# Picking the first unit's search rows with TensorE in a four-stage transformer kernel

## The chip, the core and the metric

The kernel runs on one core of a Trainium2 chip. A core has five engines, each working through its own list of instructions in order: TensorE for matrix products (PE in the profile, with its weight loads listed apart as PEld), VectorE (DVE), ScalarE (ACT), GpSimd (POOL) and SyncE (SP). In this kernel SP does nothing but issue DMA transfers, which 16 DMA engines of the core carry out. The metric is the device time of one launch in microseconds; less is better. The output has to agree with the reference.

## What is computed

A block with four residual stages on `x` of 2048 x 256:

```python
x = x + xcond0(layernorm(x), ctx, ctx, tau, delta, Wq, bq, Wk, bk, Wv, bv, Wo, bo)
x = x + top1_of_8_experts(layernorm(x), ...)
x = x + local_attention(ctx, layernorm(x), ...)
x = x + slot_layer(layernorm(x), ...)
```

The change lies in the first stage, cross attention of 2048 queries with 1601 keys in 16 heads of 16 columns:

```python
qh = (q @ Wq.T + bq).reshape(B, L, H, E)
kh = (k @ Wk.T + bk).reshape(B, S, H, E)
vh = (v @ Wv.T + bv).reshape(B, S, H, E)
scores = einsum('blhe,bshe->bhls', qh, kh) * tau + delta
a = softmax(scale * scores)
out = einsum('bhls,bshd->blhd', a, vh).reshape(B, L, D) @ Wo.T + bo
```

## The kernel before

**Units.** Queries go in 4 blocks of 512 (`LB`), heads in 4 groups of 4 (`NG`), so the attention is 16 units, each one block with one group. A unit has two passes. The *search* (`largest`, L242) finds each query's largest score by matmuls on bfloat16 copies and a VectorE maximum; the largest scores, negated and split in two parts, become two rows of the query operand. The *exact pass* (the loop of L676 to L725) then takes scores in float32r, exponentials on ScalarE, and the weighted sum. In the loop, unit `u`'s exact pass runs beside the searches of later units. Only unit 0's search has no exact pass beside it, so the loop can't start until that search has ended.

**Row operands.** Each number is split: for the search in two bfloat16 parts (`k1`, `k2`; `one_two` for queries), for the exact pass in two float32r parts (`khi`, `klo`; `hi_lo`). An operand holds three rows for each of the 16 columns of a head (high, high, low against high, low, high), four heads on the partitions in two halves (`HR` = 64) and two planes, then two rows for `delta` (`ROW_OFF`), then, in `qt`, two for the negated maximum. `kb[g]`, `qb` are the search operands and `kt[g]`, `qt`, `ql` the exact ones. A part is made with one column on each partition, so that rows have to move between partitions. All of that is done by DMA: the search parts are stored into DRAM (`store_rows`, L215: `k_rows`, `q_rows`) and fetched back in the row layout (`fetch_rows`, L225); `khi` and `klo` are copied to `kt[g]` from memory to memory on the chip, 12 transfers of 16 rows for a group (`spread`, L421); `qt` and `ql` are fetched from `q_rows` (`fill`, L225 and L504). `offsets` (L365 to L376) writes the two `delta` rows of all groups of `kb` and the four of `kt` by transfers whose destination has two or four partitions.

**Order.** The stage has its order written out by hand. SP has one queue: its transfers start in the order in which the code issues them, an instruction of SP waits for the data it sends, and it waits too until the transfer eight places ahead has landed, since eight semaphores go round. The opening is: loads; constants; layer norm of block 0; keys of columns 0 to 127 (`keys`, L390); their search parts stored; queries of the first half (L471); the rest of SP's list; then unit 0's search, 32 steps of two 402-column score tiles (matmuls L262, maximum L266). Between the steps the list `rest` is popped: queries of the second half, keys of columns 128 to 255 (`other_keys`, `more_keys`), `spread_others`, and `values` (L432, L438). After the last step `least` and `turned` (L278 to L300) put the negated maximum into `qt[0]` (the transfers `qt<-nT`, last in SP's list of the stage), and the loop's first score matmul (L720) waits for them.

**Buffers.** PSUM has eight banks: here two double tiles `two()`, one double `big()`, and one single `small()`; the eighth bank is unused until the loop's `acc`. `ew`, the expert weights, is loaded late (unit 2), and rows 12 to 15 of `x_sb` are loaded once the loop has begun.

Of the kernel before, what the change touches and what calls it, by code (L numbers as in the profile page):

```python
# [19 lines left out]
P = 128  # L20
# [42 lines left out]
def body(ctx: ExitStack, tc: tile.TileContext, a: dict, out: bass.AP):  # L63
# [3 lines left out]
    work = ctx.enter_context(tc.tile_pool(name="work", bufs=4))  # L67
# [23 lines left out]
    def layer_norm_stats(src, n, rows=P):  # L91

        stats = work.tile([P, 4, 6], F32, name="ln_stats")
        mv = work.tile([P, 4, 2], F32, name="ln_mv")
# [4 lines left out]
        ve = work.tile([P, 4], F32, name="ln_ve")  # L99
        nc.vector.tensor_scalar_add(ve[:rows, :n], mv[:rows, :n, 1], EPS)  # L100
        rstd = work.tile([P, 4], F32, name="ln_rstd")
# [38 lines left out]
    def load_experts():  # L140
# [4 lines left out]
        rev_i = work.tile([P, 1, NE], I32, name="rev_i", bufs=1)  # L145
# [33 lines left out]
    with (  # L179
# [136 lines left out]
        with tc.tile_pool(name="proj", bufs=1) as proj:  # L316
# [27 lines left out]
            nc.vector.memset(raw(qt[0]), 1.0)  # L344
            nc.vector.memset(raw(ql[0]), 0.0)
            for n in range(2):
                nc.vector.memset(qb[n], 1.0)
            nc.gpsimd.memset(v, 1.0)
# [5 lines left out]
            for n in range(1, nq):  # L354
                nc.vector.memset(raw(qt[n]), 1.0)
                nc.vector.memset(raw(ql[n]), 0.0)
# [6 lines left out]

            def offsets():
                nc.vector.tensor_scalar_mul(d, d, 0.25)  # L365
                nc.vector.memset(raw(off_t), 1.0)
                for off in (off_b, off_t):
                    nc.vector.tensor_copy(off[:, 0, :], d)
                    nc.vector.tensor_tensor(off[:, 1, :], d, raw(off)[:, 0, :], ALU.subtract)
                for rows, off in zip(off_rows, (off_t, off_b)):  # L370
                    nc.sync.dma_start(rows.rearrange("w (p j) -> p w j", p=P), raw(off))
                for rows, dst in zip(off_rows[::-1], (kb_all, kt_all)):
                    n = rows.shape[0]
                    for h in range(2):
                        r = h * HR + ROW_OFF
                        nc.sync.dma_start(  # L376
                            raw(dst[r : r + n]).rearrange("r g l s -> r (g l) s"),
                            rows[:, :SP].unsqueeze(1).to_broadcast([n, 2 * NG, SP]),
                        )
# [4 lines left out]
            k2 = proj.tile([P, SP], BF16, name="k2")  # L384

# [29 lines left out]
            def spread(g):  # L415

                for w, t in ((1, khi), (2, khi), (0, klo)):
# [8 lines left out]
            def values(i0, i1):  # L426

                ps = two()
                for i in range(i0, i1):
                    n = srows(i)  # L430
                    for c in range(2):
                        nc.tensor.matmul(  # L432
                            ps[:n, i - i0, :D], ctxT[:, c, i * P : i * P + n], wv[:, c, :],
                            start=c == 0, stop=c == 1,
                        )
                for i in range(i0, i1):
                    n = srows(i)
                    nc.scalar.copy(  # L438
                        v[:n, i, : H * VW].rearrange("p (h r) -> p h r", r=VW)[:, :, :E],
                        ps[:n, i - i0, :D].rearrange("p (h r) -> p h r", r=E),  # L440
                    )

            def block(lb):
# [23 lines left out]
                for n in range(2):  # L467
                    def project(n=n):
# [6 lines left out]
                        b = bq[:, n : n + 1]  # L475
                        for t in (one_two, hi_lo):
# [3 lines left out]
                        search, rows = q_rows[1][lb % 2][n], q_rows[0][lb % 2][n]  # L480
                        store_rows(search, slice(0, W, 2), one_two[0])
                        store_rows(search, slice(1, 2), one_two[1])
                        store_rows(rows, slice(0, 2), hi_lo[0])
                        store_rows(rows, slice(2, 3), hi_lo[1])

                    yield project

# [22 lines left out]
            first[0]()  # L510
            ps_of = [two() for _ in range(2)]
            for half in range(2):
                for part in range(2):
                    keys(0, half, part, ps_of[half])
                first_keys(0, half, ps_of[half], k1)
                second_keys(0, half, ps_of[half], k1, k2)
                store_search_keys(0, slice(half * 2 * CH, (half + 1) * 2 * CH))
            fetch_search_keys(0)
            for step in first[1:6]:
                step()  # L520
            fill_search(0)
            for half in range(2):
                first_keys(0, half, ps_of[half], khi)
            for half in range(2):
                second_keys(0, half, ps_of[half], khi, klo)
            spread(0)
            fill(0)
            fill_search(1)
            fetch_search_keys(1)
            fill(1)  # L530
            spread(1)


            rest = [first[6]]

            def other_keys(half):
                ps_of[half] = two()
                keys(1, half, 0, ps_of[half])

            def more_keys(half):  # L540
                keys(1, half, 1, ps_of[half])
# [819 lines left out]
```

## Time and profile before

| | us |
|---|---|
| median of 3 runs | 1127.58 |
| lowest, highest | 1123.11, 1133.59 |
| the profiled execution, its own time | 1131.35 |
| its span | 1129.6 |
| PE busy in the span | 964.9 (85%) |
| DVE busy | 729.0 (65%) |
| ACT busy | 501.1 (44%) |

Where the opening stands in the profiled execution, in us from the span's start:

| event | at |
|---|---|
| first key matmul (L390) | 5.89 |
| SP issues the fetch of `kb[0]` | 36.08 |
| first search matmul of unit 0 (L262) | 44.81 |
| last maximum of unit 0 | 107.17 |
| first exact matmul of the loop (L720) | 112.42 |

How to read it: the attention loop ends near 833 us and the other three stages fill the rest. A profile's row gives an operation as `out<-in`, its count and its busy time, then in brackets the idle time before it and who ended it. In a table of windows, "busy" is of the window's length, PEclk is the share of full clock that TensorE was granted, and the DMA share is the mean over the 16 DMA engines: 0.25 may mean that four of them are at work and twelve are idle.

### The profile page before, as it was taken

To read this page: it belongs to the slowest core of one execution; us is meant where nothing else is said; L and a number is where in the kernel's file an instruction comes from. 1 tells how busy PE (TensorE), PEld (TensorE's weight loads), DVE (VectorE), ACT (ScalarE), POOL (GpSimd) and SP (SyncE) were. 2 spreads that over 40 slices of the span, in tenths; PEclk is the share of its full clock that TensorE was granted. 3 is DMA by queue.
4 is the path that set the end of the run, shared out by engine and by line. 5 is a ranking of instruction groups with operands and counts; after the bars stand their busy time and mean duration, and the time that the engine had idled before them with its cause. 6 is when DMAs were issued, how large, how long until landed. Compare 5 with 4: busy or idle time off the path is not lost.

```text
span 1129.6 us, 14408 instructions
## 1 busy us (share of the span) xinstructions
PE 964.9 (85%) x5593; PEld 445.9 (39%) x5593; DVE 729.0 (65%) x1382; ACT 501.1 (44%) x579; POOL 53.5 (5%) x78
## 2 busy tenths in 40 slices
PE   5337878999988899988899999989999999998856
PEld 2114333444433344443334444343334364644524
DVE  5245667888775688867688876867025647656433
ACT  2011454666655566655566665655840011221320
POOL 1000200000010000001000000000020001011100
PEclk8568798999999899999999999998999999999765
DMA  5777212210002111010310110100043000000002
GB/s 155 160 174 140 78 43 69 59 45 26 28 1 69 42 28 27 2 26 12 100 27 2 27 27 1 28 1 1 1 115 103 1 0 1 1 1 0 1 1 74
DMA packets 33182, 47.83 MB, mean 42 GB/s; under 512 B 6530, under 2 KB 22347, under 8 KB 32859
## 3 DMA queue, kind: packets, MB, share of 16 engines
q1 hardware_dynamic: 31338, 44.48, 14.9%
q10 hardware_dynamic: 1232, 1.61, 0.4%
q0 software_dynamic: 544, 0.82, 0.3%
q8 instruction: 44, 0.72, 0.3%
q14 instruction: 24, 0.19, 0.1%
HBM read 27.66 MB, written 14.04 MB: 37 GB/s over the span
## 4 chain that ended last, share of the span: by engine, by line
PE 63%; DVE 24%; issue 5%; DMA 5%; ACT 2%; SPq 1%; POOL 0%; POOLq 0%; DVEq 0%; ACTq 0%
PE acc L676 18%; DVE mx L266 16%; PE a_ps L262 10%; PE s_ps L720 10%; PE y_ps L855 8%; PE a_ps L239 2%; DVE ln_stats L96 2%; DMA k_rows<-k 2%; PE s_ps L432 1%; PE tr_ps L816 1%; PE f_ps L1273 1%; PE s_ps L390 1%; PE o_ps L1038 1%; DVE x_sb L862 1%; PE a_ps L651 1%
## 5 line engine op out<-in xcount | busy, mean ns | idle before, releaser
L266 DVE TENSOR_REDUCE mx<-a_ps 128x1 f32<-128x402 f32 (+1 forms) x661 | 488.9, 781 | 141.3 <-PE a_ps L262 137.3
L725 ACT ACTIVATE es<-s_ps 128x1024 f32<-128x1024 f32 (+1 forms) x416 | 406.2, 1021 | 250.6 <-PE s_ps L720 237.3
L262 PE MATMUL a_ps<-kb,qb 50*128 50x402 bf16 x992 | 214.6, 346 | 72.9 <-DVE mx L266 30.8
L720 PE MATMUL s_ps<-qt,kt 52*128 52x512 f32 (+1 forms) x832 | 233.2, 519 | 2.1 <-DMA qt<-nT 2.1
L676 PE MATMUL acc<-es,v 128*32 128x512 f32 (+1 forms) x1664 | 230.5, 626 | 0.0
L262 PEld LDWEIGHTS <-qb 50*128 50x128 bf16 x1024 | 75.6, 94 | 332.6 <-issue 294.6
L720 PE MATMUL s_ps<-ql,kt 52*128 52x512 f32 (+1 forms) x832 | 187.6, 400 | 0.0
L720 PEld LDWEIGHTS s_ps<-qt,kt 52*128 52x128 f32 (+1 forms) x832 | 89.1, 187 | 50.4 <-ACT es L725 27.3
L720 PEld LDWEIGHTS s_ps<-ql,kt 52*128 52x128 f32 (+1 forms) x832 | 99.8, 189 | 0.3
L855 PE MATMUL y_ps<-expert_wT_sb,xT 128*128 128x512 f32 x192 | 89.6, 606 | 0.0
L862 DVE SCALAR_TENSOR_TENSOR x_sb<-y_ps,r_gate,x_sb 128x256 f32<-128x256 f32 x96 | 46.3, 483 | 47.4 <-PE y_ps L855 45.4
L676 PEld LDWEIGHTS acc<-es,v 128*32 128x32 f32 (+1 forms) x1664 | 33.3, 109 | 50.0 <-issue 48.4
L102 POOL TENSOR_TENSOR ln_rstd<-ln_ve,mhalf 128x4 f32<-128x4 f32 (+1 forms) x17 | 17.5, 1032 | 700.1 <-DVE ln_ve L100 700.1
L819 ACT COPY xT<-tr_ps 128x512 f32<-128x512 f32 x22 | 12.7, 584 | 84.9 <-PE tr_ps L816 84.9
L855 PEld LDWEIGHTS y_ps<-expert_wT_sb,xT 128*128 128x128 f32 x192 | 35.3, 194 | 35.5 <-issue 34.0
L625 DVE RECIPROCAL rec<-a_ps 128x16 f32<-128x16 f32 x16 | 4.1, 257 | 52.2 <-PE a_ps L239 52.2
L855 PE MATMUL y_ps<-expert_wT_sb,xnT 128*128 128x512 f32 x64 | 32.4, 633 | 0.0
L816 PE MATMUL tr_ps<-ident,xn 128*128 128x128 f32 x88 | 20.3, 330 | 12.6 <-DVE xn L107 12.3
L314 DVE SCALAR_TENSOR_TENSOR qp<-a_ps,cols,qp 128x512 bf16<-128x512 f32 x8 | 6.0, 751 | 32.8 <-ACT qhi L310 32.8
L862 DVE SCALAR_TENSOR_TENSOR x_sb<-y_ps,gate,x_sb 128x256 f32<-128x256 f32 x32 | 15.4, 482 | 13.4 <-PE y_ps L855 12.8
L816 PEld LDWEIGHTS tr_ps<-ident,xn 128*128 128x128 f32 x88 | 13.0, 159 | 27.0 <-DVE xn L107 15.3
L310 ACT ACTIVATE qp<-a_ps,cols 128x512 bf16<-128x512 f32 x8 | 5.5, 687 | 40.3 <-PE a_ps L471 40.3
(288 smaller groups left out, 689.1 us busy)
## 6 DMA issues: line engine op xcount, KB each, us to landing
qt<-q_rows SPq DMA_DIRECT2D x32, 192.0 KB
q_rows<-qhi SPq DMA_DIRECT2D x8, 512.0 KB
kt<-khi SPq DMA_DIRECT2D x32, 100.5 KB
qb<-q_rows SPq DMA_DIRECT2D x32, 96.0 KB
kb<-k_rows SPq DMA_DIRECT2D x8, 301.5 KB
q_rows<-qp SPq DMA_DIRECT2D x8, 256.0 KB
q_rows<-qlo SPq DMA_DIRECT2D x8, 256.0 KB
ql<-q_rows SPq DMA_DIRECT2D x32, 64.0 KB
```

The source lines that it names most:

```text
L96: nc.vector.bn_stats(stats[:rows, i, :], src[:, i, :])
L102: nc.gpsimd.tensor_tensor(rstd[:rows, :n], ve[:rows, :n], mhalf[:rows, :n], ALU.pow)
L239: nc.tensor.transpose(ps[:, t * P : (t + 1) * P], src[:, t, c * P : c * P + n], ident)
L262: nc.tensor.matmul(ps[:, k, :CH], qb[u % 2][rows, pl, t * P : (t + 1) * P], kb[g][rows, pl, c * CH : (c + 1) * CH], start=True, stop=True,)
L266: nc.vector.tensor_reduce(flat[:, n : n + m], ps[:, :m, :CH], AX.X, ALU.max)
L676: nc.tensor.matmul(acc[HP * j : HP * (j + 1), :], v[:n, i, h * VW : h * VW + HP], es[j // 2][:n, j % 2, :], start=i == 0, stop=i == NS - 1,)
L720: nc.tensor.matmul(ps[:n, h, :], kt[u % NG][rows, pl, i * P : i * P + n], q[u % nq][rows, pl, :], start=k == 0, stop=k == 1,)
L725: nc.scalar.activation(e[:n], ps[:n], AF.Exp)
L816: nc.tensor.transpose(ps[:, t * P : (t + 1) * P], xn[:, t, c * P : (c + 1) * P], ident)
L819: nc.scalar.copy(xT[:, c, :], ps)
L855: nc.tensor.matmul(ps.rearrange("p e d -> p (e d)"), xT[:, c, tok], ew[:, c, pair * 2 * D : (pair + 1) * 2 * D], start=c == 0, stop=c == 1,)
L862: nc.vector.scalar_tensor_tensor(xb[:, t, :], ps[:, k, :], gate[:, t, e : e + 1], xb[:, t, :], ALU.mult, ALU.add,)
```

## The change

Unit 0's `kb[0]` and `qb[0]` no longer go through DRAM. TensorE picks their rows: a constant 0/1 matrix (`pick`, one for each part and plane, made from the identity) is multiplied with `k1` and `k2`, and with the two parts of the queries, in one PSUM tile; a two-row matrix adds the `delta` rows from `off_r`. ScalarE or VectorE copies the tile out as bfloat16. Plane 0 of `kb[0]` and both planes of `qb[0]` are made before the search, plane 1 between its steps.

Second parts are, in several places, made by TensorE and ScalarE in place of VectorE: `take` multiplies a first part by minus the identity and adds it into the PSUM tile that still holds the product, and ScalarE reads what is left (`all_parts`, `rest_of_first`, `seconds_of_first`, `other_parts`).

The other work beside the search is cut into single banks: `single()` takes the eighth bank and `small()` in turn, so `two()` is left to the search; keys of the second half and values are made one bank at a time; and one item of `rest` is popped after every step, 30 in all. `khi` and `klo` of the second half have buffers of their own, in the idle space of `ew`. `pick` and the two bfloat16 identities lie in the idle rows of `x_sb`.

SP's list: the stores of the search keys stay (two instead of four), the `kb[0]` and `qb[0]` fetches go, and the `delta` rows of the operands are fetched later and in parts (`fetch_offsets`): `kt[0]` and `kb[1..3]` after `fill(0)`, `kt[1..3]` after `spread(1)`. Constants of `qt` and `ql` are written by GpSimd, and `v`'s constant after the first layer norm. The layer norm's small tiles have one buffer up to the end of attention, and four after; `si` and `bn` share one.

```diff
-    work = ctx.enter_context(tc.tile_pool(name="work", bufs=4))
+    work = [ctx.enter_context(tc.tile_pool(name="work", bufs=1))]
...
-            nc.vector.memset(raw(qt[0]), 1.0)
-            nc.vector.memset(raw(ql[0]), 0.0)
-            for n in range(2):
-                nc.vector.memset(qb[n], 1.0)
-            nc.gpsimd.memset(v, 1.0)
+            nc.gpsimd.memset(qb[1], 1.0)
+            for n in range(nq):
+                nc.gpsimd.memset(raw(qt[n]), 1.0)
+                nc.gpsimd.memset(raw(ql[n]), 0.0)
...
+            nc.vector.memset(pick, 0.0)
...
+            for k, ws in enumerate(((0, 1), (2,), (0, 2), (1,))):
+                for w in ws:
+                    for pl in range(2):
+                        nc.vector.tensor_copy(
+                            picked[:, k, pl, :, w : W * E : W],
+                            from_ident[:, :, pl * E : (pl + 1) * E],
+                        )
...
+            nc.vector.tensor_scalar_mul(less_f, ident, -1.0)
+            nc.vector.tensor_scalar_mul(less_b, ident, -1.0)
+            nc.vector.tensor_copy(more_b, ident)
...
-                for rows, dst in zip(off_rows[::-1], (kb_all, kt_all)):
-                    n = rows.shape[0]
-                    for h in range(2):
-                        r = h * HR + ROW_OFF
-                        nc.sync.dma_start(
-                            raw(dst[r : r + n]).rearrange("r g l s -> r (g l) s"),
-                            rows[:, :SP].unsqueeze(1).to_broadcast([n, 2 * NG, SP]),
-                        )
+                nc.sync.dma_start(off_r, off_rows[1][:, :SP])
+
+            def fetch_offsets(rows, dst, g0, g1):
+                n = rows.shape[0]
+                for h in range(2):
+                    r = h * HR + ROW_OFF
+                    nc.sync.dma_start(
+                        raw(dst[r : r + n, g0:g1]).rearrange("r g l s -> r (g l) s"),
+                        rows[:, :SP].unsqueeze(1).to_broadcast([n, 2 * (g1 - g0), SP]),
+                    )
...
+            khi_of = khi, idle[:, 0:SP].bitcast(F32R)
+            klo_of = klo, idle[:, SP : 2 * SP].bitcast(F32R)
...
+            def take(ps, weights, part, stop=True):
+                nc.tensor.matmul(
+                    ps, weights, part, start=False, stop=stop, skip_group_check=True
+                )
+
+            def all_parts(ps, b):
+                for t in (one_two, hi_lo):
+                    first_part(t[0], ps, b)
+                take(ps, less_b, one_two[0])
+                first_part(one_two[1], ps, b)
+                take(ps, more_b, one_two[0], False)
+                take(ps, less_f, hi_lo[0])
+                first_part(hi_lo[1], ps, b)
+                store_queries(0, 1)
...
+            def single():
+                turns.append(0)
+                if len(turns) % 2:
+                    return ps_x.tile([P, LB], F32, tag="px", name="x_ps")
+                return small()
+
+            def pick_piece(c, pl):
+                ps = single()[:, :CH]
+                s0 = c * CH
+                for k, t in enumerate((k1, k2)):
+                    nc.tensor.matmul(
+                        ps, pick[:, k, pl, :], t[:, s0 : s0 + CH], start=k == 0, stop=False
+                    )
+                nc.tensor.matmul(ps, pick_off, off_r[:, s0 : s0 + CH], start=False, stop=True)
+                nc.scalar.copy(kb[0][:, pl, s0 : s0 + CH], ps)
...
+            def pick_queries(ps, b):
+                first_part(one_two[0], ps, b)
+                second_part(one_two[1], one_two[0], ps, b)
+                kept_q.append((ps, b))
+                pick_keys(1, 0, True)
+                to = big()
+                for pl in range(2):
+                    for k in range(2):
+                        nc.tensor.matmul(
+                            to[:, pl, :], pick[:, 2 + k, pl, :], one_two[k],
+                            start=k == 0, stop=k == 1,
+                        )
+                nc.scalar.activation(qb[0][:, 0, :], to[:, 0, :], AF.Identity, bias=ones)
+                nc.vector.tensor_scalar_add(qb[0][:, 1, :], to[:, 1, :], ones)
...
-            fetch_search_keys(0)
-            for step in first[1:6]:
-                step()
-            fill_search(0)
...
+            store_search_keys(0)
+            first[3]()
+            first[4]()
+            pick_keys(0, 0, False)
+            first_keys(0, 0, ps_of[0], khi)
+            second_keys(0, 0, ps_of[0], khi, klo)
+            first[5]()
+
+            def rest_of_first():
+                first_part(hi_lo[0], *kept_q[0])
+                first_keys(0, 1, ps_of[1], khi)
+                take(kept_q[0][0], less_f, hi_lo[0])
+                first_part(hi_lo[1], *kept_q[0])
+                store_queries(0, 0)
...
+            def fetch_first():
+                fill(0)
+                fetch_offsets(off_rows[0], kt_all, 0, 1)
+                fetch_offsets(off_rows[1], kb_all, 1, NG)
+                fill_search(1)
+                fetch_search_keys(1)
+                fill(1)
+                spread(1)
+                fetch_offsets(off_rows[0], kt_all, 1, NG)
+
+            rest = [
+                rest_of_first,
+                seconds_of_first,
+                *(lambda c=c: pick_piece(c, 1) for c in range(4)),
+                fetch_first,
+                first[6],
+            ]
...
-            rest += [lambda i=i: values(i, min(i + 2, NS)) for i in range(0, NS, 2)]
+            rest += [lambda i=i: values(i) for i in range(NS)]
...
-                if 1 < n and n % 3 and rest:
+                if rest:
                     rest.pop(0)()
...
+    work[0] = ctx.enter_context(tc.tile_pool(name="work4", bufs=4))
```

## The prediction

> **What bounds the kernel now.** I read the slices of the page first, then the chain of waits up to 140 us, then SP's timeline, the waits of SP and ScalarE, and windows of two and ten us. The page's slices show one stage unlike the rest:
>
> ```profile
> PE   5337878999988899988899999989999999998856
> DMA  5777212210002111010310110100043000000002
> ```
>
> Up to slice 4 (113 us) TensorE is partly idle while the DMA engines are busy; afterwards TensorE is near full. Of the time to 140 us the chain gives its first place to a DMA:
>
> ```profile
> by line: DMA k_rows<-k 12.4%; DVE mx L266 11.4%; PE s_ps L432 11.1%; PE s_ps L390 9.5%; SPq L421 5.3%; DMA qt<-q_rows 5.1%; PE acc L676 4.0%; SPq L225 3.5%; DMA q_rows<-qp 3.4%; issue 3.3%; DMA kt<-klo 3.1%; PE a_ps L262 3.0%; DMA bo<-in_bo
> ```
>
> The waits and the timeline give it places:
>
> ```profile
> SPq L225 <- DMA k_rows<-k: 16.6, 1, 16.6
> SPq L215 <- ACT k L310: 9.2, 1, 9.2
> SPq L300 <- ACT nT L296: 8.3, 1, 8.3
> ACT khi L310 <- DMA kt<-klo: 11.7, 1, 11.7
> ...
> 36.08 0.80 SPq L225 DMA_DIRECT2D kb<-k_rows  x2
> 43.16 5.05 SPq L421 DMA_DIRECT2D kt<-khi  x8
> 79.23 2.54 SPq L215 DMA_DIRECT2D k_rows<-k  x2
> 101.11 1.07 SPq L225 DMA_DIRECT2D kb<-k_rows  x2
> 110.53 2.50 SPq L300 DMA_DIRECT2D qt<-nT  x4
> ...
> 44.81 0.76 PE L262 MATMUL a_ps<-kb,qb 50*128 50x402 bf16 x2 [20.33 <-DMA qb<-q_rows]
> 112.42 1.42 PE L720 MATMUL s_ps<-qt,kt 52*128 52x512 f32 x2 [2.08 <-DMA qt<-nT]
> ```
>
> So unit 0's search stands still until 44.8 for the trip of its rows through DRAM, stops again for 11.7 us because ScalarE may not overwrite `khi` while `spread(1)` reads it, and ends late enough that SP, through with its list at 102.2, waits 8.3 us for it. Three things can set the loop's start: the search, SP's list, and what lies ahead of `nT` on the DMA engines. Today the first does, with 8 us to the second.
>
> **The part that the loop start inherits.** From 44.8 on the DMA engines are nearly full, and before that they are not:
>
> ```profile
> 24.00:26.00 2.00, 0.48 (x1) 0.00 (x0) 0.18 (x1) 1.48 (x3) 0.00 (x0) 0.50 0.26 45
> 30.00:32.00 2.00, 0.00 (x0) 0.00 (x0) 0.00 (x0) 0.00 (x0) 0.00 (x0) 0.50 0.23 52
> ...
> 50.00:60.00 10.00, 6.84 (x24) 2.42 (x23) 6.01 (x7) 2.19 (x3) 0.00 (x0) 0.84 0.99 186
> 60.00:70.00 10.00, 0.00 (x0) 0.00 (x0) 0.00 (x0) 0.81 (x1) 0.00 (x0) 0.50 1.05 172
> 70.00:80.00 10.00, 6.42 (x18) 2.42 (x18) 7.16 (x8) 1.85 (x3) 0.00 (x0) 0.66 0.29 108
> 90.00:100.00 10.00, 8.96 (x44) 5.76 (x42) 4.75 (x6) 2.59 (x8) 0.00 (x0) 0.98 1.00 183
> ```
>
> The last three columns are TensorE's clock, DMA share and GB/s. A share of a quarter from 22 to 34 us at 25 to 76 GB/s is the `delta` fetches of L376, on few engines; they delay `k_rows` to 36.
>
> **When the search can start after the change.** SP's and DVE's own trips, by rows of before:
> - DVE loses six memsets of 0.91 and gets a memset (about 0.5), 12 casts of 32 columns and seven small constants. The 13-column cast took 0.18; with its start that is 0.2 each, so 2.4 + 1.4. It begins with `cols` at about 2.9 (SP's wait for it ends there) in place of 5.08, scales `wk` near 4.2, and is through with constants near 8.4, against 10.05. GpSimd's memsets end before it is wanted for the norm (seven of 0.88 by the 3.22 of `v`: about 8).
> - Keys wait for `ctxT`, whose load SP sees landed near 5.3, so TensorE gains 0.5 us: 16 passes of 8.6 end near 13.9. The norm now stands ahead of the second `k2` (1.05) and comes 3 us earlier: `xn` near 14.5, both transposes and copies (17 to 20.6 before) by 17.5, `k2` complete at 16.
> - New on the path: 6 bfloat16 matmuls (0.17 to 0.26 each by L262), copy 1.0, query projection 1.7 to 3.8 (L471 at half clock), first part 0.69, second 0.75, 6 more matmuls and a 0.93 copy, 4 matmuls, 0.69 and 0.75. Laid end to end from 17.5 with the overlaps that the order allows, the first search matmul is at 27.5 (26 to 31). Before: 44.8. `off_r` costs two short trips of about 3.3 us (L371 to L376) from 9.1 and is there by 15.7, hidden behind transposes; if it were late it would add itself.
>
> **How long the search takes.** 32 maxima of 0.98 at a spacing of 0.91 are 29 us. Beside them TensorE has to do, at full clock: 64 search matmuls (0.17: 11), 12 picks and 9 takes (0.2: 4), keys 16 passes of 0.34 (5.4), queries 4 of 0.43 (1.7), values 52 passes of 0.25 (1.99 for eight: 13), in sum 35. In-order waits come on top: `all_parts` has TensorE wait for three ScalarE activations in turn (about 3 us uncovered), `other_keys` makes DVE wait for keys, two activations and its 0.57 subtraction (four times 1.4), and the thirteen values steps are TensorE's, 1.35 each. My sum is 7.5 for steps 0 to 6, 4.5, 15.6 for eight keys steps, 17.5 for values, 3 for the rest: 48 us, so the search ends near 76. At half clock it would be 72 us and end at 100. `khi` of its own removes the 11.7 wait, and the 9.2 of SP with it. The end of the search thus moves by 31 us, and I don't believe the loop follows it.
>
> **What is late next: SP's list.** `nT` stays the last of the list. `spread(0)` needs `klo`, by way of two takes and four activations behind the query's, and starts near 29.6, against 43.2. From there before needed 26.7 us for 40 transfers (43.2 to 69.9) and 22.9 for 34 (79.2 to 102.2), with DMA share 0.94 to 1.05, so the list runs at the pace of the engines. That is 49.6; landing of the last took to about 106.7. Without `delta` work and without idle time in the middle, SP would be at `nT` at 29.6 + 50 + six issues of 0.3 = 81.5.
>
> **A rule against this.** The quarter share shows that the `delta` fetches occupy four engines: (0.25+0.26+0.27+0.22+0.23+0.23+0.09) x 2 us x 16 engines / 4 = 12.4 us on each from 22 to 36, part of it `k_rows` held behind them, and about 3 more before 22. The Trainium skill, "DMA: Bandwidth & Descriptors", section "Why a DMA increments its semaphore by 16 and not by 1", states that a transfer from SP uses the largest number of engines up to 16 that divides the slowest dimension of both sides, and the lowest-numbered ones. The row agrees with four; no row here shows which. By the rule the `kt` rows use engines 0 to 3, the `kb` rows 0 and 1, and `nT` (two rows) 0 and 1 as well. Before, that was paid ahead of the search; now it is put into the middle of a full list. Counted as an average over 16 engines, 13 us on four are 3 us: `nT` at 84.5, landed at 87, gain 25. By the rule engines 0 and 1 have 13 (10 to 17) us more than the others, SP can run only eight transfers ahead (about 5 us), the gap of 8.3 isn't there to absorb it, and `nT` queues behind it: SP at `nT` near 81.5 + 13 - 3 = 91.5, landed 5 us later since eight transfers stand before it: 97 (92 to 104). I take the rule's end, since transfers of 16 rows leave a share near 1.0 and so no room for those two engines to catch up.
>
> Before, `nT` had landed at 112.3. **The loop starts 15 us earlier (8 to 20).**
>
> **After the start.** The loop's instructions, and the later stages', stand in the same order on every engine. The first layer norm after attention now also waits for transfers up to the last `nT` of attention, which lies over 100 us back: 0. One buffer for the norm's tiles costs 0, as its uses are units apart. `acc` waits for the last values copy (done by then): 0. `WoT`, `bo` and `x` follow `nT` in SP's list as before and move with it. TensorE is idle ahead of the loop in both kernels, so the half clock at its start (0.50 in 110 to 120) stays. Sum: 1131.35 - 15 = 1116.4; the profiled execution stands 3.8 above the median of 1127.58, so the median becomes 1112.6, and I say 1113.
>
> **Rivals.**
> - *The extra work spreads or is absorbed* (the two engines drain the 2 KB and 3 KB pieces faster while others idle, or SP's waits cover it): gain 21 to 28, 1100 to 1107. For it: at 18 to 20 us the stores reached 351 GB/s against 160 to 190 in the full stage. Against: the share near 1.0. 0.2.
> - *The few-row fetches cost more than before* because each row now waits among other packets: 18 us or more, and a search started 3 us later: gain 3 to 8, 1120 to 1125. 0.2.
> - *Slower:* the search becomes the bound through TensorE's clock and in-order waits. The Trainium skill, "TensorE: Matmul & The Clock Gate", Part 1, has half clock after an idle window of about 3.4 us; here 70 to 90 us had 0.66 to 0.68 though TensorE was busy 6.4 to 6.8 of 10, so gaps of a step can keep it cold. At half clock the search takes 72 us with the waits counted once; it decides from (112 - 28) / 32 = 2.6 us a step. If each step also waits out a cold matmul, an activation and a maximum one after another (0.7 + 0.7 + 1.0, and the values' 1.9), a step is 2.8: search end 118, start 122, 1137. For it: 13 values and 8 keys steps have this shape. Against: 0.98 clock in 90 to 100 us with just these values steps, at 2.0 a step. 0.07.
> - *Nothing changes* because something else holds the loop's start: nothing seen but `nT`. 0.03.
>
> **The numbers.** The main case has 0.5: 1108 to 1120. Three runs of before spread over 10 us, so 1% (11 us: below 1116.3) is about what can be told from no change. Main case mostly below that (0.38 of its 0.5), the absorbed case wholly, the costly one not: faster 0.6, same 0.32, slower 0.08. To leave out 2 in 10 the range reaches from 1102, inside the absorbed case, to 1124, inside the costly one.
>
> **What would show it.** First search matmul at 26 to 31 and maxima closer than 2 us on average: steps one and two. Then last maximum well ahead of `nT`, ScalarE's `nT` copy long done when SP issues `qt<-nT`, SP waiting on transfers eight back right after the `delta` fetches, and a share below 1 there with a tail: step three. I am wrong if `qt<-nT` again waits for ScalarE (the search is the bound), or if SP reaches it before 86 or after 102.

## The result, and the profile after

The changed kernel takes 1114.62 us (median of 18 runs, 1110.37 to 1124.0), the kernel before 1124.86 in 18 runs beside it (the three runs shown earlier had 1127.58). The ratio is 0.9913, 95% interval 0.9889 to 0.9938: 10 us less. The time lies in the forecast's range, 2 us from its 1113. The gain does not come as near: 10 us where the forecast had 15. With 0.9% it falls just short of the 1% that the forecast asked for to call a result faster; it had given "faster" a chance of 0.6 and "same", which came, 0.32. That the time came out so near is in part luck, since the three runs from which the forecast started stood 2.7 us above the 18. The profiled execution took 1113.72 (span 1111.4).

| us from the span's start | before | forecast | after |
|---|---|---|---|
| keys begin on TensorE | 5.89 | about 5.4 | 7.95 |
| first search matmul | 44.81 | 27.5 | 28.22 |
| `spread(0)` begins on SyncE | 43.16 | 29.6 | 30.60 |
| search's last maximum ends | 108.15 | 76 | 86.78 |
| SyncE issues `nT` | 110.53 | 91.5 | 93.69 |
| loop's first score matmul | 112.42 | 97 | 100.90 |

The slices of the page of the changed kernel (40 slices of 27.8 us) answer to those shown of before: counted from 0, TensorE is busier in slices 1 and 2, where the search now runs, and mostly idle in slice 3, ahead of the loop's start.

```profile
PE   5783879999987999988799999989999899998756
DMA  4878012300102001001210110100044000000002
```

The timeline of the changed kernel (start, duration, engine, line, operation, tiles; in brackets the idle time before it and its releaser):

```profile
3.17 4.46 DVE L354 TENSOR_SCALAR cols<-cols,tau 128x2 f32<-128x2 f32 x1
3.63 4.26 DVE L355 TENSOR_SCALAR WkT_h_sb<-WkT_h_sb,tau 128x512 f32<-128x512 f32 x1
6.66 0.95 POOL L350 MEMSET ql<- 128x1024 f32 x1
7.95 8.69 PE L430 MATMUL s_ps<-ctxT,WkT_h_sb 128*128 128x402 f32 x16 [7.95 <-DVE WkT_h_sb L355]
...
28.22 0.52 PE L262 MATMUL a_ps<-kb,qb 50*128 50x402 bf16 x2 [1.56 <-DVE qb L604]
30.60 5.04 SPq L462 DMA_DIRECT2D kt<-khi  x8
57.83 0.83 SPq L414 DMA_DIRECT2D kt<-off_rows  x2
88.23 0.58 ACT L296 COPY nT<-a_ps 8x512 f32<-8x512 f32 x1 [3.26 <-PE a_ps L292]
92.36 1.06 SPq L225 DMA_DIRECT2D kb<-k_rows  x2
93.69 2.54 SPq L300 DMA_DIRECT2D qt<-nT  x4
100.90 0.92 PE L875 MATMUL s_ps<-qt,kt 52*128 52x512 f32 x2 [12.43 <-DMA qt<-nT]
```

Read it from below. TensorE waits 12.43 us for `nT` to land in `qt`. ScalarE had `nT` ready at 88.81, but SyncE came to it at 93.69, and landing took another 7. So the search no longer sets the loop's start; SyncE's list does. Above, VectorE's scaling of two columns of `cols` took 4.46 us, 0.23 before, and the scaling of `wk`, next in VectorE's order, 4.26, 0.48 before. They end at 7.63 and 7.89, just after GpSimd's last memset (7.61), and the keys wait for the second.

This execution's opening was an early one. Six runs below have the same code up to the search; in their profiled executions the keys start at 7.95 too, but the first search matmul at 30.9 to 32.2 and `spread(0)` at 32.8 to 34.5. TensorE's granted clock from 20 to 30 us was 0.89 here and 0.60 to 0.74 there. What made that difference is not known. Loop starts of single executions are therefore compared with care below, and SyncE's list is measured from its own start.

Windows of ten us of the changed kernel (busy time of TensorE, weight loads, VectorE, ScalarE and GpSimd, then TensorE's granted clock, DMA share and GB/s), and one of SyncE's own waits between 40 and 100 us (in total, times, longest):

```profile
60.00:70.00 10.00, 8.10 (x26) 3.27 (x25) 6.69 (x8) 2.70 (x6) 0.00 (x0) 0.66 0.70 210
70.00:80.00 10.00, 10.00 (x46) 5.89 (x45) 7.38 (x8) 2.93 (x8) 0.00 (x0) 1.00 0.65 160
90.00:100.00 10.00, 0.00 (x0) 0.00 (x0) 0.00 (x0) 0.00 (x0) 0.00 (x0) 0.50 1.04 156
...
SPq L225 <- DMA q_rows<-qlo: 6.1, 1, 6.1
```

Behind the `delta` fetches of 57.83 the DMA share falls to 0.65 to 0.70, and SyncE stands 6.1 us for an ordinary store that has to get through it. At 90 to 100 no engine computes and the DMA engines are full.

### The profile page after: what moved, and what is told of

Its sections match the earlier page's. It is cut to its first block, busy times and chain, and to the rows that moved or that the text cites. A ratio compares the mean times of both kernels' runs of the same rounds, so it can differ in the third digit from the quotient of the medians.

```text
span 1111.4 us, 14513 instructions
## 1 busy us (share of the span) xinstructions
PE 969.2 (87%) x5631; PEld 445.8 (40%) x5631; DVE 728.3 (66%) x1391; ACT 511.1 (46%) x597; POOL 59.9 (5%) x85
## 3 DMA queue, kind: packets, MB, share of 16 engines
q1 hardware_dynamic: 30478, 43.65, 14.7%
## 4 chain that ended last, share of the span: by engine, by line
PE 65%; DVE 24%; issue 5%; DMA 2%; ACT 2%; SPq 1%; POOL 1%; POOLq 0%; ACTq 0%; DVEq 0%
PE acc L831 18%; DVE mx L266 16%; PE a_ps L262 11%; PE s_ps L875 10%; PE y_ps L1011 8%; PE a_ps L239 2%; DVE ln_stats L96 2%; PE tr_ps L972 1%; PE f_ps L1429 1%; PE a_ps L509 1%; PE o_ps L1194 1%; DVE x_sb L1018 1%; SPq L462 1%; PE a_ps L806 1%; DVE xn L107 1%
## 5 line engine op out<-in xcount | busy, mean ns | idle before, releaser
L107 DVE TENSOR_SCALAR xn<-x_sb,ln_mv,ln_rstd 128x256 f32<-128x256 f32 x64 | 23.7, 430 | 1.3 <-POOL ln_rstd L102 1.2
L96 DVE BATCH_NORM_STATS2 ln_stats<-x_sb 128x6 f32<-128x256 f32 x64 | 22.3, 411 | 0.0
```

The costliest lines, as they stand in the source:

```text
L96: nc.vector.bn_stats(stats[:rows, i, :], src[:, i, :])
L107: nc.vector.tensor_scalar(dst[:, i, :], src[:, i, :], mv[:rows, i, 0:1], rstd[:rows, i : i + 1], ALU.subtract, ALU.mult,)
```

## The experiments

Theories: A, SyncE's list and the transfers ahead of `nT` hold the loop's start, the few-row `delta` fetches with a large part; B, the search holds it; C, GpSimd's memsets hold VectorE; and, of the gain, P, the early search brought it, or K, the buffers `khi_of[1]` and `klo_of[1]` did. "Loop start" is the first score matmul of the profiled execution, "total" the median. In all the runs but one the total is the loop start plus 1012 to 1018 us, so the start tells, within a few us, what a change is worth. "List" is the time from SyncE's first `spread(0)` transfer to the end of its last fetch of `kb`, behind which only `nT` stands; it is free of an early or late opening.

| run | executions | list | loop start | total | ratio to before (95%) |
|---|---|---|---|---|---|
| before | 18 | 59.0 | 112.42 | 1124.86 | |
| changed | 18 | 62.8 | 100.90 | 1114.62 | 0.9913 (0.9889 to 0.9938) |
| before_own_khi | 19 | 50.9 | 99.28 | 1114.24 | 0.9910 (0.9890 to 0.9930) |
| shared_khi | 12 | 67.9 | 107.33 | 1123.07 | 0.9979 (0.9958 to 0.9999) |
| kt_rows_late | 4 | 55.2 | 94.62 | 1110.37 | 0.9895 (0.9844 to 0.9946) |
| kt_rows_twice | 18 | 70.7 | 111.16 | 1123.99 | 0.9997 (0.9976 to 1.0017) |
| sixteen_rows_extra | 3 | 64.5 | 102.44 | 1117.12 | 0.9942 (0.9893 to 0.9992) |
| kt_rows_late_half | 2 | 55.8 | 94.27 | 1110.71 | 0.9871 (0.9816 to 0.9925) |
| memsets_late | 12 | 60.8 | 105.46 | 1123.83 | 0.9985 (0.9959 to 1.0010) |
| memsets_after_norm | 4 | 62.6 | 94.37 | 1107.84 | 0.9861 (0.9811 to 0.9911) |
| kt_rows_late_norm | 4 | 56.9 | 89.67 | 1105.43 | 0.9825 (0.9777 to 0.9872) |
| nt_from_act | 4 | | 100.44, stops | 1161.08 | 1.0347 (1.0293 to 1.0401) |
| norm_late_nt_pool | 4 | 54.3 | 100.39 | 1112.68 | 0.9872 (0.9831 to 0.9912) |
| norm_late_spread3_late | 6 | 47.1 | 89.49 | 1102.97 | 0.9798 (0.9767 to 0.9829) |

### Which part brought the gain

**before_own_khi**: the kernel before, with one part of the change.

```diff
+            idle = ew.rearrange("p c n -> p (c n)")
+            khi_of = khi, idle[:, 0:SP].bitcast(F32R)
+            klo_of = klo, idle[:, SP : 2 * SP].bitcast(F32R)
...
-                for w, t in ((1, khi), (2, khi), (0, klo)):
+                hi, lo = khi_of[g // 2], klo_of[g // 2]
+                for w, t in ((1, hi), (2, hi), (0, lo)):
```

(`more_keys` and the last subtraction take index 1 likewise.)

> The kernel before with this one part of the change: the second half of the keys gets its own hi and lo buffers (in the idle expert weights). No picks, no early search: it starts at 44.8 as before. Theory P (the picks carry the gain): ScalarE's stop of 11.7 us goes but most of it turns into SyncE's list, loop start 107 to 112, total within 5 us of before. Theory K (the stop in the middle was as costly as the trip of the rows, since SyncE's list is the next bound anyway): the second k_rows store leaves near 70 instead of 79.2, the list ends near 94 instead of 102.2, the last maximum comes near 96 instead of 107, and the loop starts near 101 (98 to 104), as early as in the changed kernel, total near 1113 to 1116.

Measured: loop start 99.28, as early as with the whole change, and the total too, with overlapping intervals. The timeline of this run:

```profile
43.69 0.74 PE L262 MATMUL a_ps<-kb,qb 50*128 50x402 bf16 x2 [20.89 <-DMA qb<-q_rows]
42.14 5.04 SPq L425 DMA_DIRECT2D kt<-khi  x8
92.01 1.07 SPq L225 DMA_DIRECT2D kb<-k_rows  x2
96.79 0.57 ACT L296 COPY nT<-a_ps 8x512 f32<-8x512 f32 x1 [6.30 <-PE a_ps L292]
97.39 2.50 SPq L300 DMA_DIRECT2D qt<-nT  x4
99.28 1.41 PE L724 MATMUL s_ps<-qt,kt 52*128 52x512 f32 x2 [2.07 <-DMA qt<-nT]
```

The search starts 15 us later than in the changed kernel and SyncE's list 11.5 us later (42.14 against 30.60), but SyncE has emptied the list at 93.1, as early as there. K holds. What sets the start in this kernel is the search: SyncE, through at 93.1, waits 4.2 us for `nT`. With its search as late as it ran here it could not start the loop sooner, however short the list; the starts near 90 further down need the early search too. That is read from these rows, no run tried it.

**shared_khi**: the changed kernel with that part undone.

```diff
-            khi_of = khi, idle[:, 0:SP].bitcast(F32R)
-            klo_of = klo, idle[:, SP : 2 * SP].bitcast(F32R)
+            khi_of = khi, khi
+            klo_of = klo, klo
```

> The changed kernel with its own hi and lo buffers for the second half of the keys taken back: both halves use khi and klo again, all else (picks, early search, single banks, memsets) stays. Theory K (those buffers carry the gain, the picks next to none): the second half's activation has to wait for spread(1) to be read, near 57, so steps other_keys stop for 8 to 12 us, the second k_rows store moves from 63.98 to 74 to 77, SyncE reaches nT near 104 to 107 and the loop starts at 108 to 114 instead of 100.9; the total is that of the kernel before within 5 us (1120 to 1127). Theory P (the picks and the early search carry it): SyncE's list has room, loop start 101 to 104, total 1114 to 1118.

Measured: 107.33, a little less than K expected; the total is nearly that of before. Waits and timeline of this run:

```profile
ACT khi L310 <- DMA kt<-klo: 7.7, 1, 7.7
SPq L215 <- ACT k L310: 19.6, 3, 14.7
...
77.70 2.50 SPq L215 DMA_DIRECT2D k_rows<-k  x2
102.99 2.50 SPq L300 DMA_DIRECT2D qt<-nT  x4
107.33 0.89 PE L875 MATMUL s_ps<-qt,kt 52*128 52x512 f32 x2 [4.53 <-DMA qt<-nT]
```

ScalarE stops for `spread(1)` and SyncE waits up to 14.7 us for the keys; the second `k_rows` store leaves 13.7 us later than in the changed kernel. From 112.42, everything else alone gives 5.1, the buffers alone 13.1, and both 11.5. By the totals, everything else alone gives only about 0.2% (the profiled execution of shared_khi was its fastest), the buffers alone 0.9%, and both 0.9%. So with the buffers there, the early search adds nothing that can be seen.

### What held the loop's start in the changed kernel

**kt_rows_late**: the four-row fetches of units 1 to 3 behind `nT`.

```diff
                 spread(1)
-                fetch_offsets(off_rows[0], kt_all, 1, NG)
...
             nc.sync.dma_start(bo, a["bo"].partition_broadcast(P))
+            fetch_offsets(off_rows[0], kt_all, 1, NG)
```

> The changed kernel with the delta fetches of four rows for units 1 to 3 (two transfers issued at 57.83, between spread(1) and the second k_rows store) moved behind the load of bo, so behind nT; those of unit 0 and the two-row fetches stay. Theory A with few-row fetches on few engines, as the prediction took it: the engines that they and nT share have about 10 us less to do, SyncE reaches nT near 89 to 91 (not 93.69), nT lands in 2 to 4 us and the loop starts at 91 to 94. If the fetches spread over all engines they are about 0.3 MB at 165 GB/s, 2 us: SyncE near 92, start near 99. Theory B (search bound): 100.9 unchanged.

Measured: 94.62, though this execution's list began 2.7 us later than the changed kernel's. The list takes 55.2 us for 62.8, SyncE is through with it at 88.53, and the wait of 6.1 us for `q_rows` is gone; now SyncE waits 1.9 us for `nT`, so list and search end together. The total's interval still overlaps that of the changed kernel.

**kt_rows_late_half**: the same, with half the search left out.

```diff
+                if u == 0 and i >= 16:
+                    nc.vector.memset(flat[:, n : n + m], 30.0)
+                    return
```

> The kernel with the four-row fetches behind bo, and unit 0's search cut to its first 16 of 32 steps (the other 32 maxima are set to a constant by VectorE, so unit 0's shift is not the reference's). It shows the list's own limit. If the search is the bound there: nT is copied near 82, and if SyncE's list were no limit the loop would start near 86. As I read the trace, the list is right behind: SyncE reaches nT at 88.5 to 89 and the loop starts at 91 to 93. Theory B (the search alone): 86 or earlier.

```profile
80.72 0.57 ACT L299 COPY nT<-a_ps 8x512 f32<-8x512 f32 x1
87.84 1.06 SPq L225 DMA_DIRECT2D kb<-k_rows  x2
89.00 2.50 SPq L303 DMA_DIRECT2D qt<-nT  x4
94.27 0.94 PE L878 MATMUL s_ps<-qt,kt 52*128 52x512 f32 x2 [13.31 <-issue]
```

The timeline of this run: `nT` is ready 9 us earlier and the loop starts no earlier (for the wait of 13.31 us the profile names no releaser; of what the matmul reads, `nT` is issued last). Even without the late fetches the list allows no start before 94 here; the 91 to 93 expected was too low, since `nT` is issued at 89.00 and the loop starts 5.3 later. B falls.

**kt_rows_twice** and **sixteen_rows_extra**: the same 302 KB more at the same place, in four-row and in sixteen-row transfers.

```diff
                 fetch_offsets(off_rows[0], kt_all, 1, NG)
+                fetch_offsets(off_rows[0], kt_all, 1, NG)    (kt_rows_twice)
...
+                for h, pl in ((0, 0), (0, 1), (1, 0)):       (sixteen_rows_extra)
+                    f = h * HR + (2 + pl) * E
+                    nc.sync.dma_start(
+                        raw(kt[1][h * HR + 1 : h * HR + W * E : W, pl, :]), raw(khi[f : f + E, :])
+                    )
```

> The changed kernel with the two four-row delta fetches for units 1 to 3 (150.8 KB each) issued twice, one pair behind the other. Few engines (they and nT share engines that the rest leaves no room on): taking the pair away made SyncE's list 4.9 us shorter and the loop start 6.3 us earlier or more, so adding one makes the loop start 5 to 10 us later, 106 to 111. All sixteen engines: the bytes alone, 302 KB at 160 to 170 GB/s, 1.8 us: 102.7.

> The changed kernel with the same bytes more at the same place, but in sixteen-row transfers: three of spread(1)'s (100.5 KB each) are issued again behind the four-row fetches. If only bytes and the number of transfers count, it costs what the doubled four-row fetches cost. If the number of rows decides over how many engines a transfer spreads, it costs 1.8 us by the bytes: loop start at 102.5 to 103.5, against 106 to 111 for the doubled four-row fetches.

SyncE's waits, the timeline and one window of kt_rows_twice:

```profile
SPq L414 <- DMA kt<-off_rows: 10.9, 2, 6.9
...
34.52 5.04 SPq L462 DMA_DIRECT2D kt<-khi  x8
62.31 12.34 SPq L414 DMA_DIRECT2D kt<-off_rows  x4
104.21 1.05 SPq L225 DMA_DIRECT2D kb<-k_rows  x2
111.16 1.04 PE L876 MATMUL s_ps<-qt,kt 52*128 52x512 f32 x2 [18.91 <-DMA qt<-nT]
...
66.00:74.00 8.00, 6.61 (x22) 2.50 (x21) 4.43 (x6) 2.32 (x5) 0.00 (x0) 0.61 0.23 37
```

and the timeline of sixteen_rows_extra:

```profile
32.81 5.04 SPq L462 DMA_DIRECT2D kt<-khi  x8
61.19 1.78 SPq L676 DMA_DIRECT2D kt<-khi  x3
96.27 1.08 SPq L225 DMA_DIRECT2D kb<-k_rows  x2
102.44 1.04 PE L880 MATMUL s_ps<-qt,kt 52*128 52x512 f32 x2 [9.93 <-DMA qt<-nT]
```

The loops start 10.3 and 1.5 us later than in the changed kernel, but the lists of these executions also began 3.9 and 2.2 us later. Measured from its own start, the list is 70.7 us with the four-row bytes and 64.5 with the sixteen-row ones, for 62.8: 8 us against 2. The totals say much the same, 9 us against 2 or 3, the second from three executions only. While little but the four-row fetches runs (66 to 74 us), the DMA share is 0.23 and 37 GB/s move: a quarter of the engines' time, as if four of 16 were at work. So bytes and the number of transfers do not decide, and the few rows are the likely cause, as the prediction took it. The two fetches differ in more than rows, though: the four-row ones read the same rows of DRAM again and again, the sixteen-row ones read `khi` on the chip. No run separates that.

### The memsets

**memsets_late** moves seven of GpSimd's memsets behind that of `v`; **memsets_after_norm** puts all eight behind a small addition that reads `xn`.

```diff
-            nc.gpsimd.memset(qb[1], 1.0)
-            for n in range(nq):
-                nc.gpsimd.memset(raw(qt[n]), 1.0)
-                nc.gpsimd.memset(raw(ql[n]), 0.0)
...
+            after_norm = proj.tile([P, 4], F32, name="after_norm")    (memsets_after_norm)
+            nc.gpsimd.tensor_tensor(after_norm, xn[:, TPB - 1, 0:4], mhalf, ALU.add)
             nc.gpsimd.memset(v, 1.0)
+            nc.gpsimd.memset(qb[1], 1.0)
...
```

> The changed kernel with GpSimd's seven memsets of qb, qt and ql moved behind its memset of v. Theory C (those memsets hold VectorE's scaling of wk and with it everything behind): wk is scaled near 4.3 and keys start near 5.4 instead of 7.95, first search matmul near 26 instead of 28.22, spread(0) near 28.3 instead of 30.60, and as the list starts earlier the loop start moves along, to 98.5 (2.4 less). If it is the load of wk or the clock that holds the keys: 7.95 stays. If the DMA engines' pace later in the list eats the lead: keys at 5.4 and loop start within 0.7 of 100.9.

> The changed kernel with all eight GpSimd memsets (v, qb, qt, ql) behind a 4-column addition that reads xn, so behind the first layer norm's last result. Theory C (a GpSimd memset holds VectorE's tensor_scalar while it runs, wherever it stands): keys start at 5.97 as in the kernel with the memsets behind v, and the four xn instructions of L107, not held now, take under 2.3 us together (2.78 in the changed kernel beside v's memset, 9.67 beside all eight); first search matmul at 24.5 to 26 instead of 28.22, and the loop start moves with the list's to 97.5 to 99.5. If the early lead is lost to the DMA engines' pace, 100 to 101.

The timeline of memsets_late, then that of memsets_after_norm:

```profile
5.97 8.06 PE L425 MATMUL s_ps<-ctxT,WkT_h_sb 128*128 128x402 f32 x16 [5.97 <-DMA ctxT<-in_ctxT]
13.31 9.67 DVE L107 TENSOR_SCALAR xn<-x_sb,ln_mv,ln_rstd 128x256 f32<-128x256 f32 x4
20.91 0.96 POOL L628 MEMSET ql<- 128x1024 f32 x1
```

```profile
12.66 1.38 DVE L107 TENSOR_SCALAR xn<-x_sb,ln_mv,ln_rstd 128x256 f32<-128x256 f32 x4
23.83 0.52 PE L262 MATMUL a_ps<-kb,qb 50*128 50x402 bf16 x2 [1.56 <-DVE qb L599]
94.37 0.89 PE L876 MATMUL s_ps<-qt,kt 52*128 52x512 f32 x2 [10.32 <-DMA qt<-nT]
```

The first move freed the keys (5.97, when `ctxT` lands) and put the hold onto `xn`: one of its four instructions took 8.71 us where the others took 0.40. My expectation had not asked what the memsets would hold in their new place. The list began 7.5 us later than in the changed kernel (38.15), the loop 4.6, and the median is 9 us higher. Behind `xn` nothing is held: the four take 1.38, the search starts at 23.83, and the loop at 94.37. That is 6.5 earlier, more than the 1.4 to 3.4 expected: the start of the list accounts for 4.4 (26.20 against 30.60), and against the 32.8 to 34.5 at which most executions with the changed kernel's opening began it, for all of it. The median is 7 us below the changed kernel's, with intervals that still overlap.

**kt_rows_late_norm** takes both cures.

> Both: the four-row fetches for units 1 to 3 behind bo, and the memsets behind the norm. There the loop started at 94.62 with the search as the bound (nT copied at 89.92, SyncE ready at 88.54). Theory A and C: the search and the list both start 2.5 to 3 us earlier, so nT is copied near 87 and the loop starts at 91 to 92.5, total 3 us less than with the late fetches alone (about 1107). If the search's steps are set by the DMA pace or a cold clock, no gain: 94 to 95.

Measured: `nT` copied at 84.18, loop start 89.67, 2 us better than expected. It is faster than the changed kernel: the intervals of the two ratios do not meet, which neither cure alone reached.

### nT by another queue

**nt_from_act** and **norm_late_nt_pool**: unit 0's `nT` issued by ScalarE in the changed kernel, and by GpSimd in kt_rows_late_norm.

```diff
-                        nc.sync.dma_start(
+                        (nc.sync if u else nc.scalar).dma_start(    (nc.gpsimd in the other)
```

> The changed kernel with unit 0's four nT transfers issued by ScalarE instead of SyncE. Theory A (SyncE's list and the transfers standing ahead of nT in its queue hold the loop's start): ScalarE issues nT right behind its copy, near 88.8, not at 93.69; if the 7.07 us of landing were a queue behind kb's fetches in SyncE's own rings, it lands in about 2 and the loop starts near 91 (10 us earlier, total 0.9 per cent less); if the DMA engines themselves are that far behind, it lands in about 7 and the loop starts near 96 (5 earlier). Theory B (the search, its in-order waits or anything else but nT holds the start): the first score matmul stays at 100.9 and the total within 2 us.

> The kernel with the late four-row fetches and the memsets behind the norm, with unit 0's nT transfers issued by GpSimd, whose transfers have completion semaphores apart from the eight that SyncE and ScalarE share, so no SyncE transfer waits for them. In its base nT is copied at 84.18 to 84.75, SyncE issues it at 84.78 and the loop starts at 89.67. GpSimd issues one transfer in 0.54, so the four leave by 87.0, as late as SyncE's by 87.3. If the 4.9 us to the first score matmul are transfers ahead in SyncE's own queue, the loop starts near 88 to 88.5; if it is the engines that are behind, 89.5 to 91, no gain.

Both theories missed the first. SyncE's waits, its timeline, and a window of nt_from_act:

```profile
SPq L225 <- DMA qt<-nT: 50.1, 3, 46.5
...
46.96 1.00 SPq L225 DMA_DIRECT2D qb<-q_rows  x2
94.50 1.40 SPq L225 DMA_DIRECT2D kb<-k_rows  x2
...
60.00:70.00 10.00, 6.87 (x22) 2.77 (x22) 5.35 (x7) 3.36 (x6) 0.00 (x0) 0.84 0.00 0
```

SyncE stands 46.5 us for `nT`, and no byte moves from 50 to 90. I read it so: in this program the transfers of SyncE and ScalarE take the same eight completion semaphores in a turn fixed when the program is built; `nT` had been given its turn before the fetch of `kb[1]`, which then had to wait for it. The wait itself is on record, and it is gone in norm_late_nt_pool, where GpSimd issues `nT`. All that stood behind came some 47 us late, and the loop, begun at 100.44, stood from 105 to 129 for its next operands. The run has one use for the search: with the DMA engines empty it took 59.3 us (30.90 to 90.21), beside nearly full ones in the changed kernel 58.6 (28.22 to 86.78), so no slowing by the transfers is seen.

In norm_late_nt_pool SyncE waits for no such turn, and this time `nT` itself lands late:

```profile
87.52 2.33 POOL L300 DMA_DIRECT2D qt<-nT  x4 [62.06 <-ACT nT L296]
102.82 0.79 PE L876 MATMUL s_ps<-qt,kt 52*128 52x512 f32 x1 [1.67 <-DMA qt<-nT]
...
90.00:100.00 10.00, 0.00 (x0) 0.00 (x0) 0.00 (x0) 0.00 (x0) 0.00 (x0) 0.50 1.15 98
```

SyncE, freed of `nT`, had already issued `x`, `WoT`, `bo` and the four-row fetches (83.93 to 88.37), and `nT`'s last piece landed over 12 us after its issue. That is far above the 88 to 91 expected for the loop's start. Likely `nT` stood behind those loads, from which SyncE's order had protected it; what GpSimd's own way of issuing adds was not tried with the engines free.

**norm_late_spread3_late**: kt_rows_late_norm, with unit 3's transfers behind `bo` too.

```diff
-                for g in (2, 3):
-                    spread(g)
-                    fetch_search_keys(g)
+                spread(2)
+                fetch_search_keys(2)
...
             fetch_offsets(off_rows[0], kt_all, 1, NG)
+            spread(3)
+            fetch_search_keys(3)
```

> The kernel with the late four-row fetches and the memsets behind the norm, and unit 3's own transfers (spread(3) and the fetch of kb[3], 14 in all, wanted only three units later) also moved behind bo, and so behind nT. In its base the search and SyncE's list end together (84.2 and 83.4) and nT lands 4.9 us after its first issue. Theory A: nT is issued near 84.8 as before, the search being the bound, but it finds the engines nearly free and lands in about 2, so the loop starts at 86.5 to 87.5 (2 to 3 us earlier than 89.67), total near 1103. If the landing of nT is not a matter of what stands ahead of it: 89.5 to 90 again. If the transfers put behind it collide with bo and the loads of x, the start is early but the next 20 us give it back.

```profile
87.00 0.57 ACT L296 COPY nT<-a_ps 8x512 f32<-8x512 f32 x1 [3.50 <-PE a_ps L292]
87.60 2.50 SPq L300 DMA_DIRECT2D qt<-nT  x4
89.49 1.34 PE L877 MATMUL s_ps<-qt,kt 52*128 52x512 f32 x2 [2.08 <-DMA qt<-nT]
```

The landing fell from 4.9 to 1.9 us as expected, but in this execution the search, unchanged in code, ended 2.8 us later (TensorE's clock in 60 to 70 us was 0.53), so the loop start is the same. Its median of 1102.97 is the lowest of all; its interval overlaps that of kt_rows_late_norm, so a gain from this last step is not shown. Against the changed kernel (0.9913) it is.

## Why the prediction was right, point by point

- **SyncE's list is the next bound: right, and shown.** Cutting the search in half moved nothing, and a longer list, a shorter one or one begun earlier each moved the loop's start, until the search became the later of the two. SyncE reached `nT` at 93.69 (91.5 forecast; 1.0 of the 2.2 came with the later `spread(0)`), and landing took 7.07 where the sum had about 5.
- **The few-row fetches cost far more than their bytes: right, and somewhat less than forecast.** The sum put 13 us on the shared engines in all; of that I later gave the four-row pair of units 1 to 3 about 10. A second pair lengthened the list by 8, taking the pair away shortened it by 6 to 8 (62.8 to 55.2, 62.6 to 56.9), and the same bytes in sixteen rows took 2. The whole list still took the 62 us of the forecast (29.6 to 91.5), so other parts of it were longer than summed. The rule that the forecast weighed, from the Trainium skill, "DMA: Bandwidth & Descriptors", section "Why a DMA increments its semaphore by 16 and not by 1", would have four engines at work; the share of 0.23 agrees. It also says that they are the lowest-numbered ones; no row here shows which they are.
- **That GpSimd's memsets cost 0: wrong.** The step only asked whether they end before GpSimd is wanted for the norm. They held VectorE: the keys came 2.5 us late (2.0 of it gone in memsets_late), and `v`'s memset held the first `xn` too (1.82 us for 0.40). Cured, the loop starts 6.5 us earlier. That the first search matmul still fell at 28.22 is luck: from keys to search the forecast had 22.1 us, and it took 20.3 in this execution, but 22.9 to 24.2 in the six others with this opening, which put the search at 30.9 to 32.2, at the end of the forecast's 26 to 31 or past it. (VectorE was freed of eight memsets, not six; the sum does not use the number.)
- **The search's length: mis-sized.** 58.6 us for 48. The steps up to `all_parts` took 11.7 (7.5 in the sum), its stall 5.5 (4.5) and the eight keys steps 20.7 (15.6), with TensorE granted half to three quarters of its clock from 30 to 70 us; the values steps, at full clock from 70 to 80, took 1.34 as forecast. Because the list was later still, it cost nothing here, but it left 5 us of margin instead of 15.
- **What the gain was due to: not seen.** The sum let the list start 13.6 us earlier and paid for the `delta` fetches in it, which comes out near the truth. But before_own_khi starts its list at 42.14 and ends it at 93.1, after 51 us; the changed kernel needs 63 from 30.60. The head start of the early search is spent in the longer list: 6 to 8 of the 12 us go to the four-row pair moved into it, the rest (SyncE's waits for unit 0's `delta` fetches and for the second keys are in it) was not split by a run. What remains is what two buffers give alone. The forecast had the number for this (9.2 us of SyncE's waiting behind `khi`) and named it in a clause, but never made the sum for that part by itself.
- **The rivals.** Absorbed: no, by the doubled fetches. More costly than before: no, 6 to 8 us for the pair. Slower, by the search: it took 1.83 us a step (58.6 / 32), under the 2.6 from which it would have decided. After the start nothing changed but the few us that other executions differ by.

## What to carry to other kernels

When a change has several parts, make the sum for each part alone against the next bound: here two spare buffers gave all that was measured, and the large part paid only once the next bound had been moved too. Before work is moved into a queue, ask how few rows it has and what stands behind it there; and before it is moved to GpSimd, ask which VectorE instructions run beside it, in its new place too.

## What the hardware showed unexpectedly

- **GpSimd memsets hold VectorE through a whole row of them.** The scaling of `cols` took 4.46 us for 0.23, with `wk`'s behind it, and one `xn` instruction 8.71 for 0.40; they ended within 0.3 us of the last memset of the row. Not all instructions are held: beside the same memsets in memsets_after_norm the cast of `kb` from the accumulators took 1.00, the subtraction into `klo` 1.05, as without them, and in the kernel before VectorE's own memsets took 0.91 beside GpSimd's and without it. The Trainium skill, "SBUF — State Buffer", section "Who interferes with whom", has VectorE's `tensor_scalar` and `cast`, in its two-port modes, and GpSimd exclude each other for an instruction; the trace agrees for `tensor_scalar`, and adds that back-to-back memsets let nothing in between.
- **Same bytes, some four times the price**: 302 KB more in four rows of DRAM 8 us of SyncE's list, in sixteen rows on the chip 2.
- **One late transfer can stop another queue in this program**: 46.5 us on SyncE for a transfer that ScalarE had to issue.
